# Two third-level Strassen products per half product, and token sums by adding DMAs, in a recurrent gate with a mixture of experts

## The chip, the core and the metric

One core of a Trainium2 chip runs the whole kernel in one launch. The metric is the device time of that launch in microseconds, the median of three runs. All arithmetic is in 32-bit floats.

## The reference, cut to what matters

```
xn  = layernorm(x)                               # 4 x 1024 tokens of 1024
ug  = xn * sigmoid(xn @ gate_w.T + gate_b)
s   = c * scan(b * ug) + (d + low_rank(mean(ug))) * ug
h   = silu(xn @ w1.T);  h = silu(h @ w3.T);  h = h @ w2.T
out = zeros;  for k in 0, 1:  out[top2[:, k]] += gate[:, k] * h   # expert ids 0 to 7 are the rows
x   = x + s * silu(out)
```

The scattering adds into rows 0 to 7 of the flattened tokens alone, since the indices are expert numbers. So the recurrence is needed for eight tokens only, w2 is applied after the scatter, to eight rows, and every other row of the result is a copy of x. The bulk of the work is three products: with the gate's weights (tokens of the first sequence only), with w1 and with w3 (all 4096 tokens).

## The kernel before

**Groups and products.** The tokens go in four groups `sb` of 1024. A group has a product of kind "u" (w1) and one of kind "m" (w3); group 0 also has "g" (the gate), side by side with u. Each is a 1024-cube, and it is done by Strassen's method in Winograd's form, with seven products instead of eight, at two levels and in part at a third:

- Outer level: seven products of 512-blocks, called half products here (class `Half`), numbered `i` = 1 to 7 and taken in the order 1, 2, 5, 6, 7, 4, 3 in u and 1, 5, 6, 2, 7, 4, 3 in m. Their token operands are the quarters of the activations or the sums `s1` to `s4` of them; their weight operands were summed in group 0 and written to HBM, or are raw quarters (`i` = 1, 2, 3).
- Inner level: a half product is seven products of 256-blocks, steps 0 to 6 of `Half.step`. A block tile `[128, 4, 512]` holds the four 256-blocks; `left_sums` makes the four inner token sums on POOL (`left_q`), and the four inner weight sums come from HBM by `load_kept_sum`. One full inner product is four matmul calls of 128x128 weights and 256 columns, which the trace shows as eight MATMULs.
- Third level, in u and m of groups 1 to 3 (`is_third`): step 3, the product `A[:, 1]` by `t[:, 2]`, is itself done with seven products of 128-blocks instead of eight (`Half.eighth`, in three parts, tile Y in one of two PSUM banks in turn). `token_thirds` makes its four token sums on POOL. Its weight sums are made on POOL in group 1 (`weight_thirds`), written to HBM, and loaded in groups 2 and 3 (`load_thirds`).

DVE adds every product from PSUM to the block it belongs to; ACT applies Silu; `whole` and `done` run when a quarter of a result is complete. In m of each group, DVE also normalises the next group's tokens (`norm`, 16 instructions of 128x1024, written `b<-b,bc`).

**Order.** All is one written-out order, in places: a half product takes seven places, `start[kind, sb, i]` is its first. `at(place, f)` puts work at a place; a generator's `yield n` puts its rest n places later. `run_todo` issues what is due ahead of each step, and every engine keeps the program's order, since `Pinned` fixes it. An instruction that waits therefore holds up everything behind it on its engine. SP issues almost all DMAs and holds up the later ones when it waits for a buffer. Before, POOL issues none.

**Buffers.** 20 blocks (`b` in the trace) and 24 quarter blocks (`q`) are handed out in the order in which they came free. PSUM has two banks X, one each of Z, W, Y, one for small things and two others.

**What the change touches.** `s1` to `s4` make the outer token sums; `s_engine` has them on POOL in groups 1 to 3, four 128x512 sums each, 24 of these blocks in all. Their places are set in the loop over `sb` at the end (`U` and `M` hold the starts of u and m). `load_kept` loads a weight block ten places ahead of its half product. `at_first` gives the seven steps of a half product their places: 0, 2, 4, 6.5, 8, 6, 12 for steps 0 to 6, so the last steps of one half product lie between the first ones of the next.

Of the kernel before, what the change touches and what calls it, by code (L numbers as in the profile page):

```python
# [16 lines left out]
P = 128  # L17
# [5 lines left out]
def kernel(  # L23
# [606 lines left out]
    def load_kept(kind, sb, i):  # L630
        name = {"u": "w1", "m": "w3"}[kind]
        t = block()
        sync.dma_start(t.tile, weights[name][raw[i]] if i in raw else kept[name, i])
        op_t[kind, sb, i] = t
# [142 lines left out]

    def s_engine(kind, sb):
        return pool if sb > 0 else dve


    BANKS = {("u", 0): (0, 1), ("m", 0): (0,)}

    def s1(kind, sb, n):
        eng = s_engine(kind, sb)
        a21, a22 = left[kind, sb, (1, 0)], left[kind, sb, (1, 1)]
        o = block(1 + n)
        if (kind, sb) in BANKS:
            yield from with_bank(o, a21, a22, (3, 0, 1, 2), op=ALU.add, of=BANKS[kind, sb])
        else:  # L790
            for q in (3, 0, 1, 2):
                eng.tensor_tensor(o[:, q], a21[:, q], a22[:, q], ALU.add)
                if q == 0:
                    yield 0.5
        a21.drop()
        a22.drop()
        left[kind, sb, "s1"] = o

    def s2(kind, sb, n):
        eng = s_engine(kind, sb)  # L800
        while (kind, sb, "s1") not in left:
            yield 0.25
        p, a11 = left[kind, sb, "s1"], left[kind, sb, (0, 0)]
        o = block(2 * n)
        if (kind, sb) in BANKS:
            yield from with_bank(o, p, a11, (2, 3, 0, 1), of=BANKS[kind, sb])
        else:
            for q in (2, 3, 0, 1):
                eng.tensor_tensor(o[:, q], p[:, q], a11[:, q], ALU.subtract)
                if q == 3:  # L810
                    yield 0.5
        p.drop()
        a11.drop()
        left[kind, sb, "s2"] = o

    def s4(kind, sb, n):

        eng = s_engine(kind, sb)
        while (kind, sb, "s2") not in left:
            yield 0.25  # L820
        o, a12 = left[kind, sb, "s2"], left[kind, sb, (0, 1)]
        if (kind, sb) == ("m", 0):
            yield from with_bank(o, o, a12, (2, 3, 0, 1), True, of=(0, 2))
        else:
            for q in (2, 3, 0, 1):
                eng.tensor_tensor(o[:, q], a12[:, q], o[:, q], ALU.subtract)
                yield 0.5
        a12.drop()
        left[kind, sb, "s4"] = o

    def s3(kind, sb, n):
        eng = s_engine(kind, sb)
        a11, a21 = left[kind, sb, (0, 0)], left[kind, sb, (1, 0)]
        o = block(n)
        if (kind, sb) == ("m", 0):
            yield from with_bank(o, a11, a21, (2, 3, 0, 1), of=(0, 2))
        else:
            for q in (2, 3, 0, 1):
                eng.tensor_tensor(o[:, q], a11[:, q], a21[:, q], ALU.subtract)
                yield 0.5  # L840
        a11.drop()
        a21.drop()
        left[kind, sb, "s3"] = o
# [26 lines left out]
    third_t = {}  # L870
    banks = deque([(ps_y, "Y"), (ps_w, "W")])

    def is_third(kind, sb, i):
        return sb > 0 and kind != "g"

    def cut(t):
        return t.rearrange("p (k n) -> p k n", n=P)

    def token_thirds(kind, sb, i):

        a = cut(left[kind, sb, S_OF[i]][:, 1])
        t = quarter()
        o = cut(t.tile)
        third_s[kind, sb, i] = t
        pool.tensor_tensor(
            o[:, 0:2], a[:, 1:2].to_broadcast([P, 2, P]), a[:, 0::3], ALU.subtract
        )
        yield 1
        pool.tensor_tensor(o[:, 2], a[:, 0], o[:, 1], ALU.subtract)
        pool.tensor_tensor(o[:, 3], a[:, 2], o[:, 2], ALU.subtract)  # L890

    def weight_thirds(kind, sb, i):

        name = {"u": "w1", "m": "w3"}[kind]
        b = cut(op_t[kind, sb, i][:, 2])
        t = quarter(2)
        o = cut(t.tile)
        third_t[kind, sb, i] = t
        pool.tensor_tensor(o[:, 1], b[:, 1], b[:, 0], ALU.subtract)
        yield 1  # L900
        pool.tensor_tensor(o[:, 2], b[:, 3], o[:, 1], ALU.add)
        pool.tensor_tensor(o[:, 3], b[:, 2], o[:, 2], ALU.subtract)
        yield 1
        pool.tensor_tensor(o[:, 0], b[:, 1], b[:, 3], ALU.add)
        yield 1
        keep_quarter(name, i, "t", t)

    def load_thirds(kind, sb, i):
        o = quarter()
        sync.dma_start(o.tile, kept[{"u": "w1", "m": "w3"}[kind], i, "t"])  # L910
        third_t[kind, sb, i] = o

# [16 lines left out]
    class Half:  # L929
# [33 lines left out]

        def eighth(self, n):
            key = self.kind, self.sb, self.i
            a, b = cut(self.A[:, 1]), cut(self.t[:, 2])
            S, T = cut(third_s[key].tile), cut(third_t[key].tile)
            d = cut(self.dst[:, 0])
            z, w = (1, 2) if self.rows_first else (2, 1)
            if n == 0:  # L970
                banks.rotate(1)
                home, tag = banks[0]
                self.Y = home.tile([P, 2 * Q], F32, tag=tag, name=f"Y_{self.tag}")
            ps = cut(self.Y)

            def go(o, p, q, start, stop):
                left_side, right_side = (p, q) if self.rows_first else (q, p)
                pe.matmul(
                    ps[:, o], left_side, right_side, start=start, stop=stop, skip_group_check=True
                )  # L980

            def add(o, p):
                dve.tensor_add(o, p, o)

            if n == 0:
                go(3, a[:, 0], b[:, 0], True, False)
                go(z, S[:, 1], T[:, 1], False, False)
                add(d[:, 0], ps[:, 3])
                add(d[:, 3], ps[:, z])
            elif n == 1:  # L990
                go(3, S[:, 2], T[:, 2], False, False)
                add(d[:, z], ps[:, 3])
            else:
                go(z, S[:, 3], b[:, 3], False, False)
                go(w, a[:, 3], T[:, 3], False, False)
                go(0, a[:, 2], b[:, 2], False, False)
                go(3, S[:, 0], T[:, 0], False, True)
                add(self.dst[:, 0], self.Y)
                add(d[:, w], ps[:, 3])
                third_s[key].drop()  # L1000
                third_t[key].drop()
                self.whole(0)

        def step(self, n):
# [16 lines left out]
            elif n == 0:  # L1021
                go(self.X, A[:, 0], t[:, 0], True, False)
                self.first(0, self.X)
            elif n == 1:
# [9 lines left out]
            elif n == 3 and is_third(self.kind, self.sb, self.i):  # L1034
                self.eighth(2)
            elif n == 3:
# [6 lines left out]
            elif n == 4:  # L1043
                go(self.X, s[2].tile, ts[2].tile, False, False)
                self.more(3, self.X)
                s[2].drop()
                ts[2].drop()
            elif n == 5:
                go(self.Z, s[3].tile, t[:, 3], False, True)
                self.more(1, self.Z)  # L1050
                s[3].drop()
            elif n == 6:
                go(self.X, A[:, 3], ts[3].tile, False, True)
                self.first(2, self.X)
                self.whole(2)
                ts[3].drop()
# [268 lines left out]
    for kind, sb, i, plain in line:  # L1325
# [6 lines left out]
        if is_third(kind, sb, i):  # L1332
            for n, step in enumerate((1, 5)):
                at(S + step, h.eighth, n)
            at(S - 2, token_thirds, kind, sb, i)
            at(S - 3, *((weight_thirds if sb == 1 else load_thirds), kind, sb, i))
        if kind != "g" and sb > 0:
            at(S - 10, load_kept, kind, sb, i)
            for j in range(4):
                at(S + 2 * T_AT[j] - 9, load_kept_sum, kind, sb, i, j)  # L1340

    for sb in range(NS):
        n = 2 if sb == 0 else 1
        U = {i: start["u", sb, i] for i in range(1, 8)}
        at(U[5] - (12 if sb > 1 else 7 if sb else 9), s1, "u", sb, n)
        at(U[5] - (9 if sb > 1 else 6), s2, "u", sb, n)
        at(U[7] - 10, s3, "u", sb, n)
        at(U[3] - (13 if sb == 0 else 8.6), s4, "u", sb, n)
        if sb == 0:
# [3 lines left out]
        at(M[5] - 4, s2, "m", sb, 1)  # L1353
        at(M[7] - 12, s3, "m", sb, 1)
        at(M[3] - 16, s4, "m", sb, 1)
        if sb > 0:
# [151 lines left out]
    for kind, sb, i, plain in line:  # L1508
        if kind == "m" or sb > 0:
            n3 = 6.5 if is_third(kind, sb, i) else 3  # L1510
            at_first[kind, sb, i] = [start[kind, sb, i] + n for n in (0, 2, 4, n3, 8, 6, 12)]
    steps = sorted(
# [87 lines left out]
```

## Time and profile before

| | |
|---|---|
| median of three runs | 815.72 us (815.4 to 816.82) |
| the profiled execution | 816.45 us, its span 814.6 us, granted clock 0.999 |
| group 1: u, m | 269.1 to 359.6 us, 359.6 to 443.4 us |
| group 2: u, m | 443.4 to 534.2 us, 534.2 to 619.7 us |
| group 3: u, m | 619.7 to 710.7 us, 710.7 to 794.1 us |
| POOL busy in these six | 77.89, 82.62, 67.19, 69.88, 64.52, 58.60 us |
| DVE busy in these six | 49.97, 59.40, 46.93, 59.02, 48.33, 48.17 us |
| DMA share in these six | 0.71, 0.82, 0.74, 0.82, 0.67, 0.53 |

The page gives each engine's busy time, where PE is TensorE's matmuls and PEld its weight loads, and groups of instructions with their count, busy time, the mean in ns and the idle time ahead of them. A windows view gives the busy time of each engine in a stretch. In the waits view a row names who waited for whom: total us, times, longest. In the view of DMA issues the last column is the median time from issue to landing. Tile names lose their numbers, so X_u is every X tile of kind u. The trace writes all instructions to one line, L89, that of the helper which records them.

### The profile page before, as it was taken

How to read it: one execution, taken by the hardware profiler on the slowest of the kernel's cores; microseconds unless marked ns; L12 is line 12 of the kernel's file. 1: busy time of each engine (PE TensorE's matmuls, PEld its weight loads, DVE VectorE, ACT ScalarE, POOL GpSimd, SP SyncE). 2: the span in 40 equal slices, each digit the busy share in tenths (PEclk: the TensorE clock that was granted, in tenths of full speed). 3: DMA queues.
4: the chain of work that ended last, by engine and by line, in shares of the span. 5: the costliest groups of instructions: out<-in, count | busy, mean ns of one | idle time of the engine just before them, and what ended most of it. 6: DMA issues, size and time to landing. Idle time of an engine off the chain costs nothing.

```text
span 814.6 us, 12336 instructions
## 1 busy us (share of the span) xinstructions
PE 804.0 (99%) x4337; PEld 698.3 (86%) x4337; DVE 513.9 (63%) x988; ACT 263.6 (32%) x458; POOL 642.2 (79%) x628
## 2 busy tenths in 40 slices
PE   8999999999999999999999999999999999999997
PEld 6888888888888878888888788888888788888884
DVE  5986598766488635744897246735894357656553
ACT  1245126876332228341022165421122021220111
POOL 2799796956999699799999962999498853997820
PEclk9999999999999999999999999999999999999999
DMA  9946609464988939659968967649957567766800
GB/s 336 421 180 233 232 28 359 183 245 138 401 298 284 350 123 341 257 177 389 364 222 325 372 236 263 226 177 388 368 196 291 173 221 244 229 199 203 337 1 2
DMA packets 61980, 203.95 MB, mean 250 GB/s; under 512 B 7152, under 2 KB 10464, under 8 KB 50272
## 3 DMA queue, kind: packets, MB, share of 16 engines
q1 hardware_dynamic: 61600, 202.63, 68.3%
q8 instruction: 35, 0.57, 0.3%
q10 hardware_dynamic: 320, 0.54, 0.2%
q14 instruction: 25, 0.20, 0.1%
HBM read 176.35 MB, written 43.54 MB: 270 GB/s over the span
## 4 chain that ended last, share of the span: by engine, by line
PE 89%; POOL 6%; issue 3%; DMA 2%; DVE 1%; ACT 0%; POOLq 0%; ACTq 0%
PE X_m L89 22%; PE X_u L89 20%; PE Z_m L89 11%; PE Z_u L89 11%; PE X_g L89 6%; PE Y_m L89 5%; PE Y_u L89 5%; POOL q L89 3%; PE Z_g L89 3%; POOL b L89 2%; PE acc L89 2%; PE plT L89 2%; DMA b<-in_x 2%; PE Y_g L89 1%; PE pp L89 0%
## 5 line engine op out<-in xcount | busy, mean ns | idle before, releaser
L89 POOL TENSOR_TENSOR q<-b 128x512 f32<-128x512 f32 (+2 forms) x224 | 244.0, 1106 | 53.3 <-DVE b L89 22.9
L89 ACT ACTIVATE b<-b 128x512 f32<-128x512 f32 (+1 forms) x152 | 105.3, 696 | 299.6 <-DVE b L89 289.3
L89 POOL TENSOR_TENSOR b<-b,b 128x512 f32<-128x512 f32 x120 | 152.6, 1294 | 61.5 <-PE X_u L89 30.0
L89 POOL TENSOR_TENSOR q<-b,q 128x128 f32<-128x128 f32 (+1 forms) x210 | 184.5, 892 | 8.0 <-issue 3.4
L89 PE MATMUL X_m<-q,q 128*128 128x256 f32 x448 | 106.0, 379 | 0.0
L89 PE MATMUL X_u<-q,q 128*128 128x256 f32 x432 | 102.4, 380 | 0.0
L89 PEld LDWEIGHTS X_m<-q,q 128*128 128x128 f32 x448 | 83.4, 190 | 11.3 <-issue 0.8
L89 DVE TENSOR_TENSOR b<-X_u,b 128x512 f32<-128x512 f32 x87 | 60.0, 689 | 51.4 <-PE X_u L89 49.8
L89 PEld LDWEIGHTS X_u<-q,q 128*128 128x128 f32 x432 | 80.2, 190 | 11.1 <-issue 1.2
L89 DVE TENSOR_TENSOR b<-X_m,b 128x512 f32<-128x512 f32 x88 | 60.4, 687 | 40.4 <-PE X_m L89 40.0
L89 POOL TENSOR_TENSOR q<-q,b 128x512 f32<-128x512 f32 x56 | 72.7, 1298 | 12.7 <-PE Z_u L89 12.1
L89 DVE TENSOR_TENSOR b<-b,bc 128x1024 f32<-128x1024 f32 x56 | 67.8, 1211 | 5.2 <-ACT bc L89 5.1
L89 DVE TENSOR_TENSOR b<-b,b 128x512 f32<-128x512 f32 x72 | 69.1, 963 | 3.0
L89 PE MATMUL X_u<-b,b 128*128 128x256 f32 x248 | 58.6, 380 | 0.2
L89 DVE TENSOR_TENSOR b<-Y_m,b 128x128 f32<-128x128 f32 (+1 forms) x112 | 41.4, 385 | 25.2 <-PE Y_m L89 14.8
L89 DVE TENSOR_TENSOR b<-Z_m,b 128x512 f32<-128x512 f32 x48 | 33.0, 688 | 38.1 <-PE Z_m L89 37.7
L89 DVE TENSOR_TENSOR b<-Z_u,b 128x512 f32<-128x512 f32 x47 | 32.4, 689 | 36.7 <-PE Z_u L89 35.8
L89 DVE TENSOR_TENSOR b<-Y_u,b 128x128 f32<-128x128 f32 (+1 forms) x111 | 40.9, 384 | 21.8 <-PE Y_u L89 13.2
L89 PE MATMUL Z_m<-b,q 128*128 128x256 f32 x224 | 53.1, 380 | 0.0
L89 PE MATMUL X_m<-b,b 128*128 128x256 f32 x224 | 53.0, 379 | 0.0
L89 PE MATMUL X_m<-q,b 128*128 128x256 f32 x224 | 53.0, 379 | 0.0
L89 PE MATMUL Z_m<-q,q 128*128 128x256 f32 x224 | 52.9, 379 | 0.0
(194 smaller groups left out, 1317.0 us busy)
## 6 DMA issues: line engine op xcount, KB each, us to landing
q<-w SPq DMA_DIRECT2D x168, 256.0 KB, 4.2
b<-in_w SPq DMA_DIRECT2D x36, 1024.0 KB, 14.9
b<-w_T SPq DMA_DIRECT2D x24, 1024.0 KB, 6.8
b<-in_xT SPq DMA_DIRECT2D x15, 1024.0 KB, 7.3
w<-q SPq DMA_DIRECT2D x56, 256.0 KB, 6.4
b<-in_x SPq DMA_DIRECT2D x12, 1024.0 KB, 10.2
w_T<-b SPq DMA_DIRECT2D x8, 1024.0 KB
q<-w_t SPq DMA_DIRECT2D x28, 256.0 KB, 3.9
```

What stands on the lines that cost most here:

```text
L89: r = f(*args, **kwargs)
```

## The change

In groups 2 and 3 a half product gets a second third-level product: step 5, the last token sum by `t[:, 3]`. `leaves_of` says how many there are: one in group 1, two in groups 2 and 3. `Half.third` takes the place of `Half.eighth`. Three of the seven products of a leaf go straight into a bank (phases "2" and "3", into Y and Z); the other four, a chain, go into bank W for both leaves (phases "a", "b", "c"), and DVE adds both leaves at once. The first leaf's weight sums take the unused quarter 1 of the weight block, which `load_kept` no longer loads; the second's have a quarter block and are made on DVE in group 1.

In groups 1 to 3, `s1` of u (groups 2 and 3), `s2` of u, and `s3` and `s4` of u and m are made in another way (`seeded`): ACT copies one operand, with its sign, into the new block, and a DMA that POOL issues adds the other operand to it. That is 17 of the 24 blocks; `s1` of u in group 1 and `s1`, `s2` of m stay on POOL. The places of all these, of the steps and of the loads move.

```diff
     def load_kept(kind, sb, i):
...
-        sync.dma_start(t.tile, weights[name][raw[i]] if i in raw else kept[name, i])
+        w = weights[name][raw[i]] if i in raw else kept[name, i]
+        sync.dma_start(t[:, 0], w[:, 0])
+        sync.dma_start(t[:, 2:4], w[:, 2:4])
...
+    def seeded(o, seed, sign, other, wait):
+        for q in range(4):
+            act.activation(o[:, q], seed[:, q], AF.Copy, scale=sign)
+            yield 0.5
+        while other not in left:
+            yield 0.25
+        yield wait
+        pool.dma_start(o.tile, left[other].tile, accum_op=ALU.add)
...
     def s1(kind, sb, n):
...
+        elif kind == "m" or sb == 1:
+            a21 = left[kind, sb, (1, 0)]
+            for q in (3, 2, 0, 1):
+                pool.tensor_tensor(o[:, q], a21[:, q], a22[:, q], ALU.add)
+                yield 0.25
         else:
-            for q in (3, 0, 1, 2):
-                eng.tensor_tensor(o[:, q], a21[:, q], a22[:, q], ALU.add)
...
+            yield from seeded(o, a22, 1.0, (kind, sb, (1, 0)), 1)
...
     def s2(kind, sb, n):
...
+        if kind == "u" and sb > 0:
+            a11 = left[kind, sb, (0, 0)]
+            o = block(2 * n)
+            for q in range(4):
+                act.activation(o[:, q], a11[:, q], AF.Copy, scale=-1.0)
+                yield 0.5
+            while (kind, sb, "s1") not in left:
+                yield 0.25
+            yield 3 if (kind, sb) == ("u", 1) else 4
+            p = left[kind, sb, "s1"]
+            pool.dma_start(o.tile, p.tile, accum_op=ALU.add)
...
     def s4(kind, sb, n):
...
+        elif sb > 0:
+            p, o = o, block()
+            yield from seeded(o, p, -1.0, (kind, sb, (0, 1)), 1)
+            p.drop()
...
     def s3(kind, sb, n):
...
+        elif sb > 0:
+            yield from seeded(o, a21, -1.0, (kind, sb, (0, 0)), 1)
...
-    def token_thirds(kind, sb, i):
-        a = cut(left[kind, sb, S_OF[i]][:, 1])
+    def token_thirds(kind, sb, i, leaf):
+        if leaf:
+            a = cut(left_q[kind, sb, i, 3].tile)
+        else:
+            a = cut(left[kind, sb, S_OF[i]][:, 1])
...
+    def weight_thirds(kind, sb, i, leaf):
...
+        if leaf:
+            eng, t = dve, quarter()
+            o = t.tile
+        else:
+            eng, o = pool, op[:, 1]
...
-        def eighth(self, n):
...
+        def third(self, phase):
...
+            def direct(ps, l, start):
+                a, b, T, S = sides[l]
+                go(ps[:, 0], a[:, 2], b[:, 2], start)
+                go(ps[:, c12], S[:, 3], b[:, 3])
+                go(ps[:, c21], a[:, 3], T[:, 3], False, True)
...
+            if phase == "a":
+                self.W = ps_w.tile([P, 2 * Q], F32, tag="W", name=f"W_{self.tag}")
+                w = cut(self.W)
+                for l, (a, b, T, S) in enumerate(sides):
+                    go(w[:, l], a[:, 0], b[:, 0], l == 0)
+                for l, (a, b, T, S) in enumerate(sides):
+                    go(w[:, 2 + l], S[:, 1], T[:, 1])
+                add(0, w[:, 0:n], False)
+                add(slice(c12, 4, 3 - c12), w[:, 2 : 2 + n], True)
+            elif phase == "b":
+                w = cut(self.W)
+                for l, (a, b, T, S) in enumerate(sides):
+                    go(w[:, l], S[:, 2], T[:, 2])
+                add(c12, w[:, 0:n], False)
+            elif phase == "c":
...
+                    go(w[:, l], S[:, 0], T[:, 0], False, l == n - 1)
+                add(slice(c21, 4, 3 - c21), w[:, 0:n], True)
...
+            elif phase == "2":
+                self.Y = ps_y.tile([P, 2 * Q], F32, tag="Y", name=f"Y_{self.tag}")
+                direct(cut(self.Y), 0, True)
+            elif phase == "y":
+                self.first(0, self.X)
+                o = self.dst[:, 0, 0 : 3 * P]
+                dve.tensor_add(o, self.Y[:, 0 : 3 * P], o)
+            elif phase == "3":
+                direct(cut(self.Z), 1, False)
+                dve.tensor_add(self.dst[:, 1], self.Z, self.dst[:, 1])
...
-            for n, step in enumerate((1, 5)):
-                at(S + step, h.eighth, n)
-            at(S - 2, token_thirds, kind, sb, i)
-            at(S - 3, *((weight_thirds if sb == 1 else load_thirds), kind, sb, i))
+            for phase, place in (("a", 5.2), ("b", 7.5), ("c", 8.8), ("y", 1.9)):
+                at(S + place, h.third, phase)
+            at(S - 2, token_thirds, kind, sb, i, 0)
+            if leaves_of(sb) == 2:
+                at(S + 1.5, token_thirds, kind, sb, i, 1)
+            if sb == 1:
+                at(S - 3, weight_thirds, kind, sb, i, 0)
+                at(S + 1.5, weight_thirds, kind, sb, i, 1)
+            else:
+                at(S - 9, load_thirds, kind, sb, i, 0)
+                at(S - 4, load_thirds, kind, sb, i, 1)
...
-                at(S + 2 * T_AT[j] - 9, load_kept_sum, kind, sb, i, j)
+                at(S + (2, 4, 8, 10.5)[j] - 9, load_kept_sum, kind, sb, i, j)
...
-        at(U[5] - (12 if sb > 1 else 7 if sb else 9), s1, "u", sb, n)
-        at(U[5] - (9 if sb > 1 else 6), s2, "u", sb, n)
-        at(U[7] - 10, s3, "u", sb, n)
-        at(U[3] - (13 if sb == 0 else 8.6), s4, "u", sb, n)
+        at(U[5] - (17 if sb > 1 else 7 if sb else 9), s1, "u", sb, n)
+        at(U[5] - (13 if sb > 1 else 12 if sb else 6), s2, "u", sb, n)
+        at(U[7] - (14 if sb else 10), s3, "u", sb, n)
+        at(U[3] - (13 if sb == 0 else 14), s4, "u", sb, n)
...
-        at(M[7] - 12, s3, "m", sb, 1)
-        at(M[3] - 16, s4, "m", sb, 1)
+        at(M[7] - (18 if sb else 12), s3, "m", sb, 1)
+        at(M[3] - (19 if sb else 16), s4, "m", sb, 1)
...
-            n3 = 6.5 if is_third(kind, sb, i) else 3
-            at_first[kind, sb, i] = [start[kind, sb, i] + n for n in (0, 2, 4, n3, 8, 6, 12)]
+            at_first[kind, sb, i] = [start[kind, sb, i] + n for n in (0, 2, 4.5, 1.5, 8, 6, 10.5)]
```

## The prediction

> **What bounds the kernel.** I read the page's busy table first, then who TensorE waited for, then TensorE's timeline inside one half product.
>
> ```profile
> span 814.6 us, 12336 instructions
> ...
> PE 804.0 (99%) x4337; PEld 698.3 (86%) x4337; DVE 513.9 (63%) x988; ACT 263.6 (32%) x458; POOL 642.2 (79%) x628
> ```
> ```profile
> PE Y_m L89 <- POOL b L89: 1.4, 1, 1.4
> ```
> The second line is the only wait in TensorE's waits view that lies between start-up and the closing rows. So the end is set by TensorE's work, and its pace decides what the change is worth:
>
> ```profile
> 303.75 1.89 PE L89 MATMUL Z_u<-q,q 128*128 128x256 f32 x8
> 305.48 1.89 PE L89 MATMUL X_u<-q,q 128*128 128x256 f32 x8
> ...
> 310.88 0.38 PE L89 MATMUL Y_u<-q,b 128*128 128x128 f32 x2
> 311.10 0.39 PE L89 MATMUL Y_u<-b,q 128*128 128x128 f32 x2
> 311.33 0.39 PE L89 MATMUL Y_u<-b,b 128*128 128x128 f32 x2
> 311.55 0.39 PE L89 MATMUL Y_u<-q,q 128*128 128x128 f32 x2
> ```
> Column one is the start. A full 256-wide product starts 1.73 us after the one before it; four 128-wide ones in a row start 0.2225 us apart, although each needs its own weight load. A half product in groups 1 to 3 is six full ones and seven narrow ones: 6 x 1.73 + 7 x 0.2225 = 11.92 us, as its starts show.
>
> Next, the helpers, a row per half product (start:end, length, then busy of PE, PEld, DVE, ACT, POOL, clock, DMA share, GB/s), in m of group 2:
>
> ```profile
> 546.16:558.09 11.93, 11.93 (x65) 10.69 (x63) 4.28 (x10) 2.83 (x5) 11.85 (x13) 1.00 0.96 369
> 558.09:571.62 13.53, 12.16 (x65) 10.76 (x64) 8.21 (x14) 1.18 (x2) 11.90 (x12) 1.00 1.02 408
> 571.62:583.54 11.92, 11.92 (x64) 10.68 (x63) 11.43 (x18) 0.00 (x0) 2.37 (x2) 1.00 1.03 405
> 595.46:607.40 11.94, 11.90 (x62) 10.34 (x61) 11.17 (x17) 2.38 (x4) 11.86 (x11) 1.00 0.41 125
> ```
> The clock is full. POOL is full in three rows, DVE nearly full in two, the DMA engines full in three. These are the places where a change that adds helper work can stop TensorE.
>
> **TensorE's saving.** In groups 2 and 3, 28 half products exchange one more full product for seven narrow ones: 1.73 - 7 x 0.2225 = 0.17 us each, 28 x 0.17 = **4.8 us**. Half products become 5 x 1.73 + 14 x 0.2225 = 11.75 us, and a place of the plan (a seventh) 1.68 us instead of 1.70. The Trainium skill (Perfetto Trace Analysis, Matmuls) speaks against this: "Larger matmuls are more efficient than smaller matmuls, when possible." By column the narrow ones are 3% dearer here (0.2225 against 1.73/8 = 0.216); that is in the 0.17 already.
>
> **The old stall.** TensorE's 1.4 us at 560 us stand against POOL, but POOL's token sums of that half product ended by 553. I read it as a late load of the third-level weight sums:
>
> ```profile
> 550.22 0.32 SPq L89 DMA_DIRECT2D q<-w_t  x1
> ```
> It left 9.6 us before its use, into DMA engines at 0.96 and 1.02. After the change load_thirds leaves 9 places ahead of the half product (15 us) instead of 3, the second leaf's 4 places ahead but used 5 into it. Either cause is eased (POOL loses work too), so -1.4 us; bounds -1.4 and 0.
>
> **POOL.** Before, 96 of these sums are s1 to s4 of groups 1 to 3:
>
> ```profile
> L89 POOL TENSOR_TENSOR b<-b,b 128x512 f32<-128x512 f32 x120 | 152.6, 1294 | 61.5 <-PE X_u L89 30.0 <-PE X_m L89 19.0 <-DVE b L89 10.1
> L89 POOL TENSOR_TENSOR q<-b,q 128x128 f32<-128x128 f32 x112 | 55.9, 499 | 4.4
> L89 POOL TENSOR_TENSOR q<-b 128x256 f32<-128x256 f32 x42 | 31.5, 751 | 5.7 <-PE X_u L89 5.7
> ```
> 17 blocks x 4 sums x 1.29 = 88 us leave POOL; the second leaf's token_thirds add 28 x (0.75 + 2 x 0.50) = 49 us. Per half product of groups 2 and 3 POOL then has four left sums (5.2) and two leaves (3.5), 8.7 of 11.75 us, and in m 10.4 us of s1 and s2 per group on top: 88% there, 75% in u. Nothing of this reaches the end; without the removal POOL would be above 100% in m and every excess microsecond would. Each adding DMA also takes POOL's time to issue, which no row shows: from 0.3 us (SP's issue) to 1.3 (one sum that it replaces), 17 of them, hidden in the 25%.
>
> **The adding DMAs.** 17 of 1 MB, block onto block, issued by POOL. POOL waits for ACT's copies before each (68 at the 0.63 us of its 128x512 activations, 43 us, on an engine 32% busy), and s2's also for s1's DMA. Behind such a wait queue left_sums and token_thirds of the coming half products. No row shows an adding DMA; 1 MB loads do:
>
> ```profile
> b<-in_w SPq DMA_DIRECT2D x36, 1024.0 KB, 14.9
> b<-w_T SPq DMA_DIRECT2D x24, 1024.0 KB, 6.8
> b<-in_xT SPq DMA_DIRECT2D x15, 1024.0 KB, 7.3
> ```
> Bounds 6.8 and 17.7 us (in_w's longest); I take 10, nearest to w_T, plus some for reading both operands. The tightest plan is u's s3 and s4: issued 5 places (8.4 us) before left_sums reads them. POOL then stands about 1.6 us. What TensorE needs first behind it is the second leaf's first token sum of the half product under way. left_sums is due 1.7 us into that half product, and phase "a" reads the token sum 10.2 us into it (five full products and seven narrow ones before it); POOL needs 3.3 us between (two left sums, then 0.75), so 5.2 us are spare. No stall, then, up to a landing of 8.4 + 5.2 = 13.6 us. s1 has 7 places (11.8 us) before s2 waits for it; m's s3 and s4 have 9 or more. The Trainium skill (DMA: Bandwidth & Descriptors, Anatomy of one DMA) gives 2.0 us plus bytes over 436 GB/s, an estimate of 4.4 us for 1 MiB, against this trace's 6.8 for a plain load; by it no reader would wait, and the term below would be zero.
>
> In m of groups 1 and 2 the DMA engines are full for some 30 us. load_kept loads a quarter block less and load_thirds replaces it, so the loads keep their bytes; s3's DMA is extra: 1 to 2 MB at 400 GB/s, 2.5 to 5 us for what queues beside it. The longest kept-sum load took 13.8 us with a lead of about 17. So 0 to 2 us per group; I take 0.7 in all, bounds 0 and 4.
>
> **SP.** 42 more issues from splitting load_kept, 28 second-leaf loads and 14 stores, at 0.32 to 0.43 us: 32 us over the 525 of groups 1 to 3, on a queue that mostly waits for buffers. Blocks are reused no sooner than 8 places after their last use. Nothing.
>
> **DVE.** Per half product of groups 2 and 3 the third level now writes 256, 512, 256, 512 and 384 columns, 0.42 + 0.69 + 0.42 + 0.69 + 0.55 = 2.77 us, instead of 4 x 0.29 + 0.69 = 1.83 (the last product's add was there before): +0.94 us, 26 in all. Group 1 pays +0.14, and 4 second-leaf weight sums each, 1.2 us. Normally this fills idle time. But the two full rows above become 11.43 + 0.94 = 12.4 and 12.1 us of work in 11.75, and in group 1 the like (11.55 and 11.34 busy) 12.9 and 12.7 in 11.92, by its rows from 395.51 and 419.36. DVE already runs late there: the product started at 575.52 was done at 577.25, its add began at 578.84. New waits are tighter: phase "b" writes over what phase "a"'s first add reads, 2.4 us (three narrow and one full product) later, or 2.0 net of the add; X has about 2.0 between steps 4 and 6. Lateness of 1.6 + 0.6 to 1.0 passes that by 0.2 to 0.6, at some four places: I take **+1.0 us**, bounds 0 and 4.
>
> **Tail.** Step 6 moves ahead of the last transposes: TensorE's 0.97 us wait there hides, and the first 1.85 us of output products start about as much later. 0, bounds -1 and +1.
>
> **Sum.** The profiled execution took 816.45 us (span 814.6 and 1.85 around it), 0.73 above the median of 815.72. 816.45 - 4.8 - 1.4 + 0.7 + 1.0 = 811.95; against the median, **811.2 us**.
>
> **Rivals.**
> - *Given back*: DVE or the full DMA engines cost what their bounds allow and the old stall stays in part. -4.8 + 2 to 4.4 gives 813 to 815.5. For it: the full rows. Against: each lasts two half products.
> - *The adding DMA lands after its readers* (the slower side). In u of groups 2 and 3 four of them stand ahead of the token sums. Each microsecond beyond 13.6 costs 4 us; the forecast's gain of 4.5 us is gone at a landing of 14.7, and it is slower by over 0.2% from 15.1. At 17.7 it costs 16 us: 827.6. For it: in_w's row, and two operands read at w_T's pace would be 13.6. Against: the u groups leave the DMA engines 20 to 30% free.
> - *No gain*: narrow products in runs of three and four do not keep 0.2225 us once two leaves share bank W, and 0.25 us each eats it (7 x 0.25 = 1.75): 815.5 to 816. Against: the four-run above.
>
> **Chances.** Forecast 0.55, own range 809.4 to 813.2; given back 0.18; late DMA 0.21; no gain 0.06. A measurement of this kernel can tell about 0.2%, 1.6 us: faster means under 814.1. Faster: 0.55 + 0.13 of given back = 0.68; same: 0.05 + 0.06 = 0.11; slower 0.21. The range runs from 809.2 (all terms at their good end: 815.72 - 4.8 - 1.4, and a little of the tail) to 818, which takes in given back, no gain and the lightest of the late DMAs, leaving about 0.18 out.
>
> **What would show it.** Right: half products of u and m in groups 2 and 3 start 11.75 us apart; no q<-w_t wait near 560; POOL near 605 us busy plus its issues; DVE near 560; adding DMAs landing within 12 us. Wrong: TensorE waits for POOL at phase "a" or "3" in u (late DMA), or for DVE at "b" or step 6 in m while tokens are normalised (given back), or narrow products further apart than 0.23 us (no gain).

## The result, and the profile after

The changed kernel took **841.9 us** (median of four runs, 840.2 to 847.2) against 815.9 in the same session: 1.033 times, 95% interval 1.028 to 1.038. It is slower by 26 us, where 811.2 was forecast. The profiled execution took 840.2 us.

The page's busy table of the changed kernel:

```profile
span 838.4 us, 12915 instructions
...
PE 808.5 (96%) x4505; PEld 701.5 (84%) x4505; DVE 579.2 (69%) x1044; ACT 294.9 (35%) x526; POOL 620.9 (74%) x661
```

TensorE is busy for 4.5 us more and the span is 23.8 us longer, so most of the loss is time in which TensorE stands. The waits view (us in total, times, longest), which had one line before between start-up and the closing rows, says for whom:

```profile
PE W_m L89 <- DVE b L89: 5.5, 6, 1.4
PE X_u L89 <- DVE b L89: 4.9, 5, 1.4
PE Y_m L89 <- POOL q L89: 3.9, 3, 2.0
PE W_u L89 <- DVE b L89: 3.6, 2, 2.5
PE X_m L89 <- DVE b L89: 2.4, 3, 1.7
```

16.4 us for DVE, 3.9 for POOL, in 19 waits of 0.2 to 2.5 us. None is for the third-level weight sums, as one was before at 560 us. Where nothing waits, the saving is there, as the starts of three half products in u of group 3 show:

```profile
670.15 1.89 PE L89 MATMUL X_u<-b,b 128*128 128x256 f32 x8
681.91 1.89 PE L89 MATMUL X_u<-b,b 128*128 128x256 f32 x8
693.67 1.68 PE L89 MATMUL X_u<-b,b 128*128 128x256 f32 x7
```

They are 11.76 us apart, 11.75 was forecast. In m of group 2, by half product (columns as in the prediction's rows), the undisturbed first and third stand beside the second and fourth:

```profile
548.80:560.67 11.87, 11.87 (x71) 10.74 (x70) 4.90 (x10) 3.97 (x7) 11.63 (x14) 1.00 0.18 53
560.67:574.72 14.05, 12.03 (x71) 10.81 (x69) 5.21 (x10) 4.74 (x9) 13.80 (x16) 1.00 0.96 364
574.72:586.48 11.76, 11.76 (x70) 10.73 (x69) 9.22 (x15) 2.83 (x6) 9.48 (x12) 1.00 1.04 332
586.48:600.59 14.11, 12.19 (x70) 10.62 (x68) 12.57 (x16) 0.46 (x1) 13.55 (x14) 1.00 1.05 379
```

In the last row DVE has 12.57 us of work, more than the 11.75 that there are, with POOL full beside it. What fills DVE shows in its groups by form (busy us, mean ns of one):

```profile
L89 DVE TENSOR_TENSOR b<-b,b 128x512 f32<-128x512 f32 x72 | 73.9, 1030 | 2.3
...
L89 DVE TENSOR_TENSOR b<-X_m,b 128x512 f32<-128x512 f32 x88 | 60.3, 685 | 39.5 <-PE X_m L89 39.2
...
L89 DVE TENSOR_TENSOR q<-b,q 128x128 f32<-128x128 f32 x28 | 20.0, 714 | 0.1
...
L89 DVE TENSOR_TENSOR q<-b 128x128 f32<-128x128 f32 x28 | 17.0, 607 | 0.0
```

The first two rows do the same arithmetic on the same shape. With one operand in PSUM (a bank, into which TensorE writes) it takes 685 ns, with both in SBUF (where the blocks lie) 1030. One at a time, in the timeline of groups 1 to 3: of 48 adds of two blocks the eight during which POOL was idle, or nearly, took 0.69 us each; the 36 that had POOL at work beside them for at least nine tenths of their time took 1.19 on average, at most 2.56. The second leaf's weight sums (last two rows) take 0.28 us with POOL idle, 20 of 56, and 0.87 on average beside it. The kernel before already had this: its `b<-b,b` row reads 963 ns, and 33 of its 48 such adds lay beside POOL at 1.06; but it had room for it.

One place in u of group 1 shows how the lateness reaches TensorE:

```profile
306.14 4.12 DVE L89 TENSOR_TENSOR q<-b,q 128x128 f32<-128x128 f32 x2
...
306.82 0.85 POOL L89 TENSOR_TENSOR q<-b 128x256 f32<-128x256 f32 x1
307.51 0.97 POOL L89 TENSOR_TENSOR b<-b 128x128 f32<-128x128 f32 x2
308.33 2.30 POOL L89 TENSOR_TENSOR q<-b,q 128x512 f32<-128x512 f32 x3
...
310.71 0.68 DVE L89 TENSOR_TENSOR b<-X_u,b 128x512 f32<-128x512 f32 x1
...
311.44 1.99 PE L89 MATMUL X_u<-b,b 128*128 128x256 f32 x8 [0.94 <-DVE b L89]
```

Two small weight sums hold DVE for 4.12 us, while POOL works off a row of sums; the add that frees X stands behind them, and TensorE waits 0.94 us.

The adding DMAs are as they were costed: POOL spends 0.88 us on each issue, and the landing is 10.7 us. Loads land later than before: kept sums after 7.2 us instead of 4.2, tokens after 11.6 instead of 7.3 (so late they also land in the run with POOL sums below, without adding DMAs). But TensorE waits only 0.8 us for loads:

```profile
b<-b POOLq DMA_DIRECT2D x17, 1024.0 KB, 10.7
b<-in_xT SPq DMA_DIRECT2D x15, 1024.0 KB, 11.6
```

### The profile page after: what moved, and what is told of

Read it like the earlier page. It is cut to its first block, busy times and chain, and to the rows that moved or that the text cites. A ratio compares the mean times of both kernels' runs of the same rounds, so it can differ in the third digit from the quotient of the medians.

```text
span 838.4 us, 12915 instructions
## 1 busy us (share of the span) xinstructions
PE 808.5 (96%) x4505; PEld 701.5 (84%) x4505; DVE 579.2 (69%) x1044; ACT 294.9 (35%) x526; POOL 620.9 (74%) x661
## 4 chain that ended last, share of the span: by engine, by line
PE 76%; DVE 9%; DMA 8%; POOL 3%; ACT 2%; issue 2%; SPq 0%; POOLq 0%; ACTq 0%; DVEq 0%
PE X_u L89 20%; PE X_m L89 16%; PE Z_u L89 8%; DVE b L89 7%; PE Z_m L89 6%; PE X_g L89 6%; PE W_u L89 3%; PE Z_g L89 3%; PE W_m L89 3%; DMA b<-in_xT 3%; PE Y_u L89 3%; PE Y_m L89 2%; PE acc L89 2%; ACT b L89 2%; PE plT L89 2%
## 5 line engine op out<-in xcount | busy, mean ns | idle before, releaser
L89 POOL TENSOR_TENSOR q<-b 128x512 f32<-128x512 f32 (+1 forms) x196 | 235.5, 1229 | 87.0 <-DMA b<-b 22.9
L89 ACT ACTIVATE b<-b 128x512 f32<-128x512 f32 (+1 forms) x220 | 142.1, 672 | 291.5 <-DVE b L89 284.7
L89 POOL TENSOR_TENSOR q<-b,q 128x128 f32<-128x128 f32 (+1 forms) x182 | 171.3, 965 | 17.9 <-PE X_m L89 9.1
L89 PE MATMUL X_m<-q,q 128*128 128x256 f32 x448 | 106.4, 380 | 2.6 <-DVE b L89 2.2
L89 POOL TENSOR_TENSOR b<-b,b 128x512 f32<-128x512 f32 x52 | 65.5, 1283 | 13.3 <-ACT b L89 6.7
L89 PE MATMUL Z_m<-q,q 128*128 128x256 f32 (+1 forms) x252 | 58.4, 368 | 0.0
L89 PE MATMUL Z_u<-q,q 128*128 128x256 f32 (+1 forms) x244 | 56.6, 368 | 0.0
L89 DVE TENSOR_TENSOR b<-W_m,b 128x256 f32<-128x256 f32 (+1 forms) x84 | 38.9, 483 | 21.9 <-PE W_m L89 21.0
L89 DVE TENSOR_TENSOR b<-W_u,b 128x256 f32<-128x256 f32 (+1 forms) x84 | 39.0, 484 | 20.9 <-PE W_u L89 20.1
L89 PEld LDWEIGHTS X_u<-b,b 128*128 128x128 f32 x248 | 45.9, 190 | 7.6 <-DVE b L89 1.6
L89 PE MATMUL X_u<-b,q 128*128 128x256 f32 x216 | 51.3, 381 | 0.0
## 6 DMA issues: line engine op xcount, KB each, us to landing
b<-b POOLq DMA_DIRECT2D x17, 1024.0 KB, 10.7
b<-in_xT SPq DMA_DIRECT2D x15, 1024.0 KB, 11.6
```

The costliest lines, as they stand in the source:

```text
L89: r = f(*args, **kwargs)
```

## The experiments

The theories: **A**, DVE comes late to W and X because it has more instructions and the new places leave it little room; **B**, ACT's copies and the adding DMAs hold POOL up; **C**, formed after the first runs, DVE's adds of two SBUF operands are slowed by POOL's sums, and the change puts more of both where TensorE waits next. The table gives stage lengths of the profiled executions, from the first product of a stage to that of the next (the last column to the end), and the median time.

| | u1 | m1 | u2 | m2 | u3 | m3 | us |
|---|---|---|---|---|---|---|---|
| before | 90.9 | 83.7 | 90.9 | 85.5 | 90.9 | 104.1 | 815.9 |
| after | 99.3 | 91.1 | 90.9 | 90.4 | 92.8 | 106.4 | 841.9 |
| POOL sums, one leaf | 91.3 | 85.4 | 91.6 | 84.3 | 91.6 | 104.1 | 818.3 |
| adding DMAs, one leaf | 90.6 | 86.5 | 94.3 | 86.8 | 92.7 | 107.0 | 827.3 |
| POOL sums, two leaves | 93.9 | 90.0 | 92.2 | 87.4 | 91.3 | 106.6 | 832.6 |
| the same, sums from `acc` | 90.9 | 83.7 | 90.7 | 84.2 | 89.8 | 105.2 | 814.5 |
| the same, copies to PSUM | 93.1 | 86.1 | 90.7 | 85.6 | 89.8 | 105.1 | 820.8 |

### Which part costs what

Second leaf off, adding DMAs off, or both, in the changed kernel:

```diff
# one leaf
     def leaves_of(sb):
-        return 2 if sb > 1 else 1
+        return 1
# POOL sums: s1 to s4 and their places as before
-            yield from seeded(o, a21, -1.0, (kind, sb, (0, 0)), 1)
+            for q in (2, 3, 0, 1):
+                pool.tensor_tensor(o[:, q], a11[:, q], a21[:, q], ALU.subtract)
+                yield 0.5
...
```

> The changed kernel with s1 to s4 as in the kernel before (POOL sums, no adding DMAs, no ACT copies, the old places), second leaf and all else kept. Theory B: group 1 (190.3 us in the changed kernel, 174.7 before) comes back to 175 to 179 us, and u of group 2 and 3 lose nothing; POOL is overfull in m of groups 2 and 3, which costs some us there. Theory A: group 1 stays at 186 us or more, since POOL's sums slow DVE's in the same stage as much as before; the whole 838 us or more.

> The changed kernel with one leaf in all groups (no second third-level product, no weight sums for it), the new phases, bank W and the adding DMAs kept. Theory A: group 1 gains as in the run with the weight sums on POOL or more (6 to 11 us); in groups 2 and 3 the DVE adds are 0.9 us less a half product and their waits for DVE (8 us in all) mostly go, for 4.8 us of TensorE work more: 826 to 832 us. Theory B: group 1 stays above 186 us and m of group 2 above 89 us; 840 us or more. If the phases of the first leaf alone were the cause, group 1 would stay too, with the waits at W.

> The changed kernel with POOL sums at the old places and one leaf in all groups: what stays of the change are the new phases, bank W alone for the chain, the new step places and the loads. Theory B and additive parts: 827.3 - 9.3 = 818 us. If the new layout alone (a, b 2.4 us apart in one bank, step 6 early) costs nothing: 815 to 816.5 us. If it costs with POOL's sums beside it: 820 us or more, with waits for DVE at W and X.

Measured: 832.6 with POOL sums, 827.3 with one leaf, 818.3 with both. The parts add up either way: the layout (phases, bank W, places, loads) costs 818.3 - 815.7 = 2.7 us; the second leaf 832.6 - 818.3 = 14.3 without the adding DMAs and 841.9 - 827.3 = 14.6 with them, its saving of 4.8 already in it; the adding DMAs 9.0 with one leaf and 9.3 with two. Neither A nor B alone is right. With POOL sums group 1 still took 184 us, nearer to A's 186 than to B's 175 to 179, and 15 us of waits for DVE stayed; yet the time fell by 9.3 us, as B wants, and all waits for POOL went.

The adding DMAs, put into the kernel before, then with the load of the weight sums earlier, and that load alone:

```diff
-            at(S - 3, *((weight_thirds if sb == 1 else load_thirds), kind, sb, i))
+            at(*((S - 3, weight_thirds) if sb == 1 else (S - 9, load_thirds)), kind, sb, i)
```

> The kernel before (one leaf, the old phases, Y and W in turn, old steps) with only s1 to s4 of groups 1 to 3 made as in the changed kernel: ACT copies, adding DMAs, their new places. Theory B2 (the adding DMAs cost by themselves; taking them out of the changed kernel gave 9.3 us): 821 to 826 us, with waits for POOL or DMA in TensorE's view. Theory A2 (they cost only where the new phases leave TensorE no room): 817.5 us or less.

> The kernel before with the adding DMAs, as in the run that took 824.2 us, and the load of the third-level weight sums nine places ahead in groups 2 and 3. In that run TensorE waited once, 6.5 us in m of group 2, for such a load. If the adding DMAs cost through that load alone: 815 to 817 us. If they cost also through POOL's backlogs beside DVE's adds, in the old places too: 818 us or more.

> The kernel before with the load of the third-level weight sums in groups 2 and 3 nine places ahead of its half product instead of three. The prediction read TensorE's 1.4 us wait at 560 us as this load landing late. If so the wait goes: 814.2 us. If it stood for POOL, as the view says, it stays: 815.7 us.

Measured: 824.2, 816.2 and 815.0 us. In the first, TensorE's waits view has one large line between start-up and the close:

```profile
PE Y_m L89 <- DMA q<-w_t: 6.5, 1, 6.5
```

So that price was the late load; with it gone the adding DMAs cost the old layout 816.2 - 815.0 = 1.2 us, or 0.7 by the ratios to the kernel before (0.9995 and 0.9987, each known to about 0.8 us), not 9. The load alone, moved earlier, takes the old wait at 560 us away and makes the kernel before faster: 0.9987 times, interval 0.9977 to 0.9996. This is the version that beats both.

### The weight sums on POOL

```diff
-            eng, t = dve, quarter()
+            eng, t = pool, quarter()
```

> The changed kernel with the second leaf's weight sums of group 1 (56 sums of 128x128) made on POOL instead of DVE. DVE's 56 sums take 37 us in group 1, 0.28 us each alone and up to 3.7 us beside POOL's. Theory A (DVE comes late to free banks W and X; most of it in group 1 and made by these sums): group 1, 190.3 us from 267.55 to 457.88, falls by 6 to 11 us, TensorE's waits for DVE at X_u near 337 and 350 go, the whole takes 831 to 836 us. Theory B (ACT's copies and the adding DMAs hold up POOL and ACT): group 1 stays within 2 us or grows, since POOL gets 28 us more behind its waits; 840 us or more.

Measured: 842.7 us, group 1 188.0 instead of 190.3. TensorE's waits for DVE there fell from 7.6 to 1.0 us, and it waited for POOL at Y instead, once 3.0 and once 4.4 us. Theory A's price for these sums failed as an argument: on either of the two engines they cost group 1 about the same.

### One operand from PSUM

First with `acc`, a bank that is there anyway, as the second operand, so that these blocks hold other values; then in full, with ACT's copies:

```diff
# from acc
-                dve.tensor_add(c12[:, q], c22[:, q], c21[:, q])
+                dve.tensor_add(c12[:, q], c22[:, q], acc if sb > 0 else c21[:, q])
...
-        eng.tensor_tensor(c[:, 1], b[:, 1], b[:, 0], ALU.subtract)
+        eng.tensor_tensor(c[:, 1], b[:, 1], acc[:, 0:P] if leaf else b[:, 0], ALU.subtract)
...
# in full: a bank that is free (rows in u, small things in m), filled ahead
+    def copy_ahead(kind, sb, i, q):
+        ps = bank_tile(1 if kind == "u" else 2)
+        act.copy(ps, tiles[kind, sb, "c22"][:, q])
+        ahead[kind, sb, i] = q, ps
...
+        dve.tensor_add(out[:, q], ps, c21[:, q])
```

> The changed kernel in which the 48 adds of two SBUF blocks by DVE in groups 1 to 3 (the quarters made whole in half products 6 and 7, written b<-b,b) read their second operand from the PSUM bank acc instead of a block: the same work for DVE, but one SBUF operand. These quarters then hold other values. In the changed kernel such an add takes 0.69 us with POOL idle and 1.19 us on average beside POOL's sums, at most 2.56. Theory C (DVE is late because POOL's sums slow its SBUF adds, and POOL's backlogs now fall beside them): all 48 take 0.69 to 0.72 us, TensorE's 7 us of waits at X go for the most part, 833 to 837 us. Theory A' (the number of DVE instructions and the tight places, not their slowing): at most 2 us less, 840 us or more.

> As the run with the adds from acc, and the 56 weight sums of the second leaf in group 1 (0.28 us alone, 0.80 us beside POOL, up to 3.7) read one operand from acc too; the second leaf's weight sums then hold other values. Theory C: these fall from 37 to 16 to 18 us, group 1 (190.3 us) comes to 178 to 182 us, the whole to 826 to 831 us. Theory A': group 1 stays at 187 us or more, the whole at 838 or more.

Measured: 825.5 and 819.0 us, 16.3 and 22.8 less than the changed kernel, with its adding DMAs, its places and as many DVE instructions. The DVE groups of the second run:

```profile
L89 DVE TENSOR_TENSOR b<-b,acc 128x512 f32<-128x512 f32 x81 | 55.0, 679 | 4.5 <-ACT acc L89 3.8
...
L89 DVE TENSOR_TENSOR q<-b,acc 128x128 f32<-128x128 f32 x56 | 14.3, 278 | 0.0
```

The 48 adds (here with 33 others that read `acc` anyway) at 679 ns and the 56 weight sums at 278, whatever POOL does beside them. Theory A', that the count and the places matter and not the slowing, fell by more than 10 us.

> The changed kernel with POOL sums at the old places instead of the adding DMAs, and DVE's 48 adds of whole quarters and the 56 weight sums with one operand from the bank acc (these hold other values). If the 9.3 us of the adding DMAs have a way of their own (loads, POOL's standing), they come off the 819.0 us of the run with both from acc: 809 to 812 us. If they went through DVE's slowed adds, which are gone there already: 817 to 820 us.

> The whole computation again: POOL sums at the old places, and for 48 whole quarters and 13 of 14 sets of weight sums ACT first copies one operand to a free PSUM bank, so that DVE reads one operand from PSUM (61 copies of 0.57 us, 35 us on ACT; the weight sums 2 places later). If the slowing of DVE's SBUF adds beside POOL is the main cause: the time of the run from acc with POOL sums plus 0 to 4 us for waits on ACT, 810 to 816 us. If ACT's copies come late: 818 us or more, with waits for ACT on DVE.

> The changed kernel with its adding DMAs, and the same ACT copies to PSUM banks for the whole quarters and the weight sums. If the slowing of DVE's SBUF adds is the main cause: 819 to 823 us (the run from acc took 819.0). If ACT, which also makes the 68 seeds, becomes late: 828 us or more.

Measured: 814.5, 820.8 and 823.5 us. The runs from `acc` keep every place but drop some waits on earlier results. The last two compute everything, with the second leaf's weight sums 2 places later, to give the copies time: 832.6 falls to 820.8 and 841.9 to 823.5, 18.4 of the 26 us. The doubt that one pair leaves the other does not share. The adding DMAs cost 9.3 us with slowed adds, and 4.6 (from `acc`; 5.3 by the ratios to the kernel before) or 2.7 (copies) without: four to seven tenths of their price went away with the slowed adds.

The slowing is mutual. With the same sums to do, POOL's busy time fell from 692.9 to 672.5 us without adding DMAs and from 620.9 to 603.9 with them when DVE read from PSUM; in the run with POOL sums, POOL's own 128x512 sums took 1.40 us on average beside DVE's sums of two SBUF operands and 1.28 otherwise. So some of the gain with adding DMAs may have come by way of POOL: TensorE's waits for it fell from 3.9 to 2.8 us. Without them TensorE waited for POOL in neither run. What the full version with POOL sums keeps of the loss stands mostly in group 1 and m of group 2:

```profile
PE W_m L89 <- DVE b L89: 3.4, 4, 1.5
PE W_u L89 <- DVE b L89: 1.9, 2, 1.1
```

### How an adding DMA slows DVE

> The changed kernel with every adding DMA replaced by four POOL sums at the same place (the new block, copied by ACT as before, plus the other operand). What stays are ACT's copies, their waits and the places. Theory B3 (the DMA itself: its landing, for which POOL stands, and the loads that it delays): back to about 832.6 us, the time with POOL sums at the old places. Theory B4 (POOL stands for ACT's copies, 44 us, and then works off its backlog beside DVE): 838 us or more, more so as POOL gets 68 sums of 1.3 us back.

```diff
-        pool.dma_start(o.tile, left[other].tile, accum_op=ALU.add)
+        for q in range(4):
+            pool.tensor_tensor(o[:, q], o[:, q], left[other][:, q], ALU.add)
```

Measured: 834.5 us. ACT's copies and the new places thus cost 1.9 us over the POOL sums at the old places, which is not clear of the scatter, and the DMA itself 7.4, although POOL has 73 us less to do with it. The waits of POOL, with one leaf, first with the adding DMAs:

```profile
POOL q L89 <- DMA b<-b: 55.5, 11, 8.3
POOL b L89 <- ACT b L89: 52.7, 12, 12.7
```

Work that stood behind such a wait follows in one piece. So in u of group 2: POOL waits 8.35 us and then works without a break until 510.8. The timeline of the same stretch there (the adds of half product 6) follows for both kernels with one leaf. With adding DMAs:

```profile
496.13 2.50 POOL L89 TENSOR_TENSOR q<-b 128x512 f32<-128x512 f32 x2 [8.35 <-DMA b<-b]
...
506.71 0.86 POOL L89 DMA_DIRECT2D b<-b  x1
...
507.31 1.01 POOL L89 TENSOR_TENSOR q<-b 128x256 f32<-128x256 f32 x1
...
507.68 2.83 DVE L89 TENSOR_TENSOR b<-b,b 128x512 f32<-128x512 f32 x1
508.00 2.82 POOL L89 TENSOR_TENSOR q<-b,q 128x512 f32<-128x512 f32 x3
510.54 0.69 DVE L89 TENSOR_TENSOR b<-X_u,b 128x512 f32<-128x512 f32 x1
...
511.29 1.99 PE L89 MATMUL X_u<-q,q 128*128 128x256 f32 x8 [2.05 <-DVE b L89]
```

With POOL sums:

```profile
506.05 0.69 DVE L89 TENSOR_TENSOR b<-b,b 128x512 f32<-128x512 f32 x1
...
506.77 0.69 DVE L89 TENSOR_TENSOR b<-X_u,b 128x512 f32<-128x512 f32 x1
...
508.40 1.89 PE L89 MATMUL X_u<-q,q 128*128 128x256 f32 x8
508.65 1.27 POOL L89 TENSOR_TENSOR b<-b,b 128x512 f32<-128x512 f32 x1 [13.00 <-PE X_u L89]
```

The add that makes the quarter whole takes 2.83 us beside POOL's backlog and 0.69 beside an idle POOL. In the new order of phases the add that frees X (`first(0, X)`, phase y) stands behind it and behind step 4's adds; before, it stood at step 0, ahead of step 4's.

### Looser places

```diff
# first try; y stays at 1.9, step 6 moves to 11.6
-("a", 5.2), ("b", 7.5), ("c", 8.8), ("y", 1.9)
+("a", 5.2), ("b", 8.2), ("c", 9.2), ("y", 1.9)
# second, with POOL sums: y at 2.3, step 6 at 11.6; the third is this with the weight sums on POOL
# last two: y at 2.3, step 6 stays at 10.5
```

> The changed kernel with places moved apart and no work removed: phase b at 8.2 instead of 7.5 (behind step 4), c at 9.2 instead of 8.8 (behind the next half product's y and step 1), step 6 at 11.6 instead of 10.5 (behind the next one's step 2). The gap from a to b grows from 2.4 to 4.1 us, that from step 4 to step 6 by 1.7 us. Theory A, tightness (DVE is late by 1 to 2 us now and then): of 16.4 us of waits for DVE at most 5 are left, 827 to 832 us. Theory A, throughput (DVE is late by more than any of these gaps): 836 us or more. Theory B: waits for POOL (3.9 us) stay, and so does most of the loss; 838 us or more.

> The changed kernel with both edits at once: s1 to s4 as POOL sums at the old places, and phase b at 8.2, c at 9.2, y at 2.3 (behind c), step 6 at 11.6. With POOL sums alone 832.6 us were left, with 15 us of waits for DVE at W and X. Theory A, tightness: at most 4 us of them stay, 817 to 822 us. Theory A, throughput of DVE in m: they stay, 827 us or more. Theory B (only the adding DMAs cost): 830 to 833 us, as without the loosening.

> As the run with POOL sums and loose places, and the second leaf's weight sums of group 1 on POOL too. If DVE is what is short in group 1, 2 to 5 us less than that run, all in group 1. If POOL is full there (82.6 of 83.7 us in m of group 1 before, and 14 us come), TensorE waits for POOL at Y_m in group 1 and the time is the same or up to 5 us more.

> The complete kernel with POOL sums and ACT's copies to PSUM (820.8 us), and phase b at 8.2 behind step 4, c at 9.2 behind the next half product's step 1, y at 2.3 behind c, step 6 left at 10.5, so that it lies between y and step 2. From a to b there are then 4.1 us instead of 2.4, from b to c 2.4, from y to step 2 about 1.7 us and c's products. If the 5.3 us of waits left at W come from the short way from a to b: 814 to 818 us. If DVE's lateness only moves to the next bank: 819 us or more, with waits at X where step 2 follows y.

> The changed kernel with these places alone: adding DMAs, DVE's SBUF adds as they are. The share of the short way from a to b in the 26 us: if the lateness of 1 to 2 us would pass unseen with 4.1 us, 830 to 836 us; if the slowed adds make DVE later than any gap, or it shows at X instead, 840 us or more.

Measured: 834.9, 906.8, 902.1, 826.0 and 847.9 us. In the first, y comes ahead of the c of the half product before, so that some quarters hold other values; waits for DVE fell from 16.4 to about 5 us, but those for POOL grew to 5.8. In the second and third, c and y came to stand directly ahead of step 2, which writes into the bank that y frees, and nearly every half product waited (in the second 55 us at X for DVE, 18 for ACT). The last two have step 6 between, and still lost 5.2 us against 820.8 and 6.0 against 841.9 (4.4 and 3.2 by the ratios to the kernel before; the last is within the runs' scatter). In the fourth all waits at W are gone, and they are at X:

```profile
PE X_u L89 <- DVE b L89: 4.3, 6, 0.7
PE X_m L89 <- DVE b L89: 4.1, 6, 0.7
```

Twelve waits of about one 0.69 us add each, behind half products 6 and 7, whose adds of whole quarters now stand between c and y. So room given to W is taken from X. Whether another order of the steps would give both enough is open; none tried here did, and the short way from a to b alone does not explain the loss.

## Why the prediction was wrong, step by step

- **The DVE term failed**: +1.0 us, bounds 0 and 4. It took each instruction at the duration of its row or by its columns and asked whether the sum fits a half product. The weight sums were sized at 1.2 us for four; they took 2.6 (37 us over 14 sets), and DVE's busy time, forecast near 560 us, was 579.2. More than that, durations were taken as the engine's own. Reading one operand from PSUM won back 16.3 and 22.8 us at unchanged places and 18.4 in the complete kernel, so most of the miss of 30.7 us was that these adds were priced as if POOL did not slow them.
- **POOL**: busy was right (605 and issues forecast; 620.9, of it 15.0 issues). "Nothing of this reaches the end" was wrong: at 74% busy POOL still sets how long DVE's adds of two SBUF operands take. The Trainium skill (GPSIMD Engine Reference, Key points) has a rule that spoke against the change and that I passed over: VectorE instructions with two SBUF inputs contend with GpSimd for its SBUF interfaces. The rows here agree, 0.69 us alone and 1.19 beside POOL; the page gives no size.
- **TensorE's saving** of 4.8 us was right: u of group 3 takes 89.78 us in the runs where nothing waits there, 90.93 before: 1.15 for seven half products against 7 x 0.17 = 1.19. Narrow products kept 0.2225 us. That narrow products are dearer by column cost nothing beyond the 3% already counted.
- **The old stall** was read rightly as a late load, against the releaser that the view named: moving the load alone removed it, m of group 2 went from 85.5 to 83.9 us, the median by 0.9.
- **The adding DMAs**: landing 10.7 us against 10 taken, and no wait for POOL at "a" or "3" in u. The bound of 13.6 us for a stall was asked of the wrong reader: what hurts is not who reads the block but what POOL does after standing for it. Price 9.3 us where 0.7 stood.
- **SP** at nothing held: TensorE's waits for loads are 0.8 us in all. **Tail** at 0, bound +1: TensorE now waits 1.5 us for ACT's last Silu ahead of the closing rows, 0.97 for DVE before; in the run of 814.5 us the stretch from m of group 3 to the end still took 105.2 us, where 104.1 - 1.2 = 102.9 were due, and a wait at W explains only 0.4 of it.
- **Rivals**: "given back" named DVE, with the full rows for it, and priced it at 2 to 4.4 us by the same sizing. The slower rival had the right side and the wrong mechanism.

Left open: the 3.3 us between 814.5 and the forecast's 811.2, part of it layout and the close; how much of group 1's remaining loss in the full version is ACT's copies coming late; and how much of the gain from PSUM operands, with adding DMAs, came through POOL's quicker sums.

## What to carry to other kernels

A duration from a row holds only for the neighbours it was measured beside: compare rows of the same operation and shape whose operands lie in different memories, and if one is longer, ask what runs beside it before adding work to either engine. An engine that is only 75% busy can still cost time, by when it works: a wait put into its queue turns spread work into a backlog. And an order with several operations between a product and the add that frees its bank should be checked by which of them can be late.

## What was not expected of the hardware

- DVE's 128x512 adds of two SBUF operands in groups 1 to 3 took 0.69 us with POOL idle and 0.96 to 1.35 on average beside it, by kernel (single ones up to 3.6); of those with one PSUM operand none took more than 0.70 us in any of the twenty traces.
- A longer wait can cost TensorE twice. After the 2.55 us wait at 315.98 us the granted clock (third number from the right, 1.00 in the row before) fell to 0.60 on average over 4.3 us, a loss of 1.7 us more:

```profile
313.00:316.31 3.31, 0.76 (x6) 0.36 (x4) 1.36 (x6) 3.25 (x8) 2.44 (x2) 1.00 0.98 337
316.31:320.60 4.29, 4.29 (x19) 3.81 (x18) 1.88 (x6) 3.75 (x9) 4.21 (x8) 0.60 1.02 386
```

  Over all twenty traces, between 267 us and the last product of m of group 3, 19 of 33 waits of 2.26 us or more were followed by a stretch at half clock, 3.4 us long (6.8 after the longest wait, 6.5 us), and one of the 57 waits between 1.5 and 2.2 us. The Trainium skill (TensorE: Matmul & The Clock Gate, Part 1) speaks of an idle window of about 3.4 us; here shorter waits sufficed.
- An adding DMA of 1 MB from SBUF to SBUF landed after 10.7 us, a plain load of 1 MB in the kernel before after 6.8 to 14.9.
